# Residual shifts added by accumulating DMAs, and ScalarE's copies of the fifth product placed ahead of a norm, in a two-layer graph network on one Trainium2 core

## The chip, the core and the metric

The kernel runs on one core of one Trainium2 chip. The core has five engines, each with its own instruction queue: TensorE (PE in the profile; PEld is its weight load), VectorE (DVE), ScalarE (ACT), GpSimd (POOL) and SyncE (SP), which here issues DMA transfers alone. ScalarE and GpSimd issue a few transfers as well. All engines work on the on-chip memory SBUF; TensorE writes its sums into the banks of PSUM, from which VectorE and ScalarE read.

The metric is the device time of one execution in microseconds (us), the median of several runs. Lower is better.

## What is computed

64 graphs of 256 nodes with 256 features pass through two layers. Layer 0 is a graph attention layer with two attention steps, a norm, a feed-forward block with relu and a second norm. Layer 1 is a relational attention with 8 heads, a norm, a feed-forward block with gelu and a last norm. Cut to what matters:

```python
# layer 0
h = _gat(x, adj, W1, a1, Fout)
h = _gat(h, adj, W2, a2, W2.shape[1])
h = _layernorm(residual + h, g_ln1, b_ln1)
residual2 = h
ff = jnp.matmul(jax.nn.relu(jnp.matmul(h, w_ff1) + b_ff1), w_ff2) + b_ff2
return _layernorm(residual2 + ff, g_ln2, b_ln2)
# layer 1
...
attn_out = out.transpose(0, 2, 1, 3).reshape(Bb, Nn, Dm) @ Wo + bo
x = _ln(src + attn_out, g1, beta1)
ff = jax.nn.gelu(x @ W1 + b1, approximate=False) @ W2 + b2
return _ln(x + ff, g2, beta2)
```

All is float32. Each `_layernorm` or `_ln` ends with `* g + b`: a scale and a shift for each of the 256 features.

## The kernel before

**Tiles.** Two graphs make a unit; there are 32 units. A unit's residual rows are a tile `y` of 128 partitions x 4 x 256 (four blocks `t` of 128 nodes, 512 KB). There are four such tiles, which are reused.

**The norm in three parts.** `norm` (L795) takes statistics of each block on VectorE and has GpSimd make 1/sqrt(var + eps), called `rs`. `applied_norm` (L811) makes the negative mean `nm` on VectorE and then applies both to each block, on ScalarE (L821) or, where it is told so, on GpSimd (L818). `affine` (L824) scales with `times` (L830) and shifts with `plus` (L833), each one VectorE instruction over the whole tile. The features that go on into the next matmul don't need `affine`: its scale and shift are folded into the weights. So `affine` serves the residual path alone, and `rb1`, `rb2` and `rb3` also hold the bias of the matmul that is added next. `rb4` belongs to the output.

| vectors | used on | added to the tile next |
|---|---|---|
| `rg1`, `rb1` | rows after the first norm of layer 0 | feed-forward output of layer 0 (L961) |
| `rg2`, `rb2` | rows after the second norm of layer 0 | attention output (L789) |
| `rg3`, `rb3` | rows after the first norm of layer 1 | feed-forward output of layer 1 (L961) |
| `rg4`, `rb4` | rows after the last norm | nothing: stored by SyncE (L1120) |

**The feed-forward blocks.** Each block's first matmul is done as seven products of quarters (Strassen's scheme in the form of Winograd), each in two halves `a` and `b`: `hidden_seven` (L835). A step's name is the product and the half. Products 2, 5 and 3 use one PSUM bank of their half (`h1b`), and ScalarE copies it out after each (L873); products 1, 6, 7 and 4 use another (`h1a`), which VectorE adds into the same place of `h1` (L876). Product 3 accumulates on top of 5 in the same bank, so 3 of a half waits for the copy of 5 of that half; 6 needs the copy of 3. Step `r` and `s` are the activation. The second matmul is seven products too: `HiddenOut` (L923), with quarter sums on VectorE (L939) and adds into `y` (L961).

**Turns.** `turn(y_, x_, z)` (L1144) works on three units at once: on unit `y_` in layer 1, on `x_` in the feed-forward block of layer 0, and on `z` in the two GAT steps. There are 32 turns. While three units are there, the order on TensorE, SyncE, VectorE and ScalarE is the order of the code; GpSimd's order is the scheduler's. The places that the change touches, in a turn's order:

- After the first norm of `x_` and its transposes (`normed_features`, L663), `times` with `rg1` (L1197); the shift with `rb1` comes much later (L1227), among the relu products.
- After the first norm of `y_` and its transposes: `affine` with `rg4`, `rb4` of the unit that waits to be stored, the store (`stored`, L1118), then the load of the next rows (L1281).
- The gelu products of `y_` (L1296 to L1303), with the second norm of `x_` applied in between: block 0 after `5a`, then `affine` with `rg3`, `rb3`, block 1 after `5b`, blocks 2 and 3 (on GpSimd) after `3a` and `3b`.
- After output product 3 of `y_`: `affine` with `rg2`, `rb2` of `x_` (L1337).

`normed_features` transposes 32 x 32 blocks on VectorE (L668) and then moves 16 blocks into place: four by GpSimd copies (L685, L677), twelve by transfers from SyncE, or six each from SyncE and ScalarE. At the second norm of `x_` (L1305), the transposes need all four blocks of the norm.

A check of the input at the end chooses a general path otherwise; it isn't taken here.

Of the kernel before, what the change touches and what calls it, by code (L numbers as in the profile page):

```python
# [12 lines left out]
ALU = mybir.AluOpType  # L13
# [372 lines left out]
def narrow_path(  # L386
# [13 lines left out]
    nc = tc.nc  # L400
# [102 lines left out]
    def row(v, name, t=None):  # L503
        n = v.shape[0]
        if t is None:
            t = const.tile([P, n], F32, name=name)
        nc.sync.dma_start(t, bass.AP(tensor=v.tensor, offset=v.offset, ap=[[0, P], [1, n]]))
        return t
# [41 lines left out]
    rg1, rb1, rg2, rb2 = row(g_g1, "rg1"), row(g_b1, "rb1"), row(g_g2, "rg2"), row(g_b2, "rb2")  # L550
# [10 lines left out]
    rg3, rb3, rg4, rb4 = row(t_g1, "rg3"), row(t_be1, "rb3"), row(t_g2, "rg4"), row(t_be2, "rb4")  # L561
# [101 lines left out]
    def normed_features(u, l, xn, natural=False, queues=(nc.sync,)):  # L663


        yt = work.tile([P, Q, KB, T, 32], F32, tag="yt", name=f"yt{u}_{l}", bufs=1)
        for t in range(T):
            mark["transposed"] = nc.vector.transpose(  # L668
                yt[:, :, :, t].rearrange("p q k r -> p k q r"),
                xn[:, t].rearrange("p (k q c) -> p k q c", k=KB, c=32))  # L670
        if natural:
            hT = work.tile([P, KB, TN], F32, tag="hT", name=f"hT{u}_{l}")
            to = hT.rearrange("c k (t a r) -> c (k t) a r", a=Q, r=32)
            for q in range(Q):
                for a in range(Q):
                    move = nc.gpsimd.tensor_copy if q == a else nc.sync.dma_start
                    move(to[q * 32:(q + 1) * 32, :, a], yt[a * 32:(a + 1) * 32, q].rearrange("c k t r -> c (k t) r"))  # L677
            return [hT[:, k] for k in range(KB)]
        hT = work.tile([P, Q, KB, T, 32], F32, tag="hT", name=f"hT{u}_{l}")
        n = 0  # L680
        for q in range(Q):
            for a in range(Q):
                to, at = hT[q * 32:(q + 1) * 32, a], yt[a * 32:(a + 1) * 32, q]
                if q == a:
                    nc.gpsimd.tensor_copy(to, at)  # L685
                else:
                    mark["placed"] = queues[n % len(queues)].dma_start(to, at)
                    n += 1
        return [hT[:, :, k].rearrange("p a t r -> p t a r") for k in range(KB)]
# [105 lines left out]
    def norm(u, l, y, blocks=range(T)):  # L795
        n, t0 = f"{u}_{l}_{blocks[0]}", blocks[0]
        bt = slice(t0, t0 + len(blocks))
        st = work.tile([P, T, 6], F32, tag="st", name=f"st{n}", bufs=1)
        mv = work.tile([P, T, 2], F32, tag="mv", name=f"mv{n}")
        rs = work.tile([P, T], F32, tag="rs", name=f"rs{n}")  # L800
        nm = work.tile([P, T], F32, tag="nm", name=f"nm{n}")
        for t in blocks:
            nc.vector.bn_stats(st[:, t, :], y[:, t, :])  # L803
            nc.vector.bn_aggr(mv[:, t, :], st[:, t, :])  # L804
        nc.gpsimd.tensor_scalar(rs[:, bt], mv[:, bt, 1], EPS, 0.0, op0=ALU.add, op1=ALU.add)  # L805
        nc.gpsimd.tensor_tensor(rs[:, bt], rs[:, bt], mhalf[:, bt], ALU.pow)  # L806
        if l == 3:
            nc.gpsimd.tensor_add(high[:, bt], high[:, bt], mv[:, bt, 0])
        return blocks, mv, rs, nm

    def applied_norm(y, blocks, mv, rs, nm, part=None, gpsimd=False):  # L811
        bt = slice(blocks[0], blocks[0] + len(blocks))
        if part is None or part[0] == blocks[0]:
            nc.vector.scalar_tensor_tensor(nm[:, bt], mv[:, bt, 0], -1.0, rs[:, bt],  # L814
                                           op0=ALU.mult, op1=ALU.mult)
        for t in part or blocks:
            if gpsimd:
                nc.gpsimd.tensor_scalar(y[:, t, :], y[:, t, :], rs[:, t:t + 1], nm[:, t:t + 1],  # L818
                                        op0=ALU.mult, op1=ALU.add)
                continue  # L820
            mark["normed"] = nc.scalar.activation(y[:, t, :], y[:, t, :], AF.Identity,  # L821
                                                  bias=nm[:, t:t + 1], scale=rs[:, t:t + 1])

    def affine(y, g_, b_):  # L824

        times(y, g_)
        plus(y, b_)

    def times(y, g_):
        nc.vector.tensor_mul(y, y, g_[:, None, :].to_broadcast(list(y.shape)))  # L830

    def plus(y, b_):
        nc.vector.tensor_add(y, y, b_[:, None, :].to_broadcast(list(y.shape)))  # L833

    def hidden_seven(u, l, hT, w, bi, func, d, tt):  # L835

# [281 lines left out]
    def stored(u, y, bt):  # L1118
        b = slice(G * u + bt.start // NB, G * u + bt.stop // NB)
        nc.sync.dma_start(out[b].rearrange("b (c p) f -> p (b c) f", p=P), y[:, bt, :])  # L1120

    def finish(u, y, b):

        normed(u, 3, y, range(b * NB, (b + 1) * NB))
        bt = slice(b * NB, (b + 1) * NB)
        affine(y[:, bt, :], rg4, rb4)
        stored(u, y, bt)
# [16 lines left out]
    def turn(y_, x_, z):  # L1144
        Y, X, Z = (g.get(u) for u in (y_, x_, z))
        hT, y = Y["hT"], Y["y"]
# [7 lines left out]
        def scores(n):  # L1154
            e[n] = weighted(y_, *quads[n], q, k_, Y["aT"])
# [20 lines left out]
        def first(names, ends=0):  # L1176

            if X:
                steps(names)
            else:  # L1180
                for _ in range(ends):
                    piece()
# [4 lines left out]
        with order:  # L1187
# [6 lines left out]
            key(1)  # L1194
            if X:
                X["hT"] = normed_features(x_, 0, X["y"])
                times(X["y"], rg1)  # L1197
            scores(0)
            if z + 1 < NG:
                load_x(z + 1)  # L1200
# [22 lines left out]
            first("5b 7a 3b ra 6b")  # L1223
            totals(2)
            first("4a 7b rb")
            if X:
                plus(X["y"], rb1)  # L1227
            scores(3)
            first("sa sb", 2)
            masks(3)  # L1230
# [19 lines left out]
            n = norm(y_, 2, y)  # L1250
# [16 lines left out]
            if X:  # L1267
                out(6)
                hT = normed_features(y_, 2, y, queues=(nc.sync, nc.scalar))
                out(3)  # L1270
                out.sums(3)
            else:
                piece()
                hT = to_features(y, f"h3T{y_}")
                hT = [h.rearrange("p (t a r) -> p t a r", t=T, r=32) for h in hT]
                affine(y, rg3, rb3)
            if waiting:
                affine(waiting[0][1], rg4, rb4)
                stored(*waiting.pop(), slice(0, T))
            if z + 1 < NG:  # L1280
                load_rows(z + 1)  # L1281
# [9 lines left out]
            second = hidden_seven(y_, 1, hT, w1s, b1, AF.Gelu, Y, tt.rearrange("p a n -> p (a n)"))  # L1291
            if X:
                out.add(4)
                n = norm(x_, 1, X["y"])
            h1 = Y["h1"] = work.tile([P, FB, TN], F32, tag="h1", name=f"h1{y_}_1", bufs=1)
            second("2a 1a 2b 1b")  # L1296
            for t, name in enumerate(("5a", "5b", "3a", "3b")):
                second(name)
                if X:
                    applied_norm(X["y"], *n, [t], t > 1)  # L1300
                if X and t == 0:
                    affine(y, rg3, rb3)
            second("6a 6b ra rb 7a 7b")  # L1303
            if Z:
                X["hT"] = normed_features(x_, 1, X["y"], natural=True)  # L1305
# [28 lines left out]
            Z["m"].shares()  # L1334
            Z["m"].scaled(F)
            out(3)
            affine(X["y"], rg2, rb2)  # L1337
            out(7)
            checked(z, Z["aq"])
            if z + 1 < NG:  # L1340
# [6 lines left out]
    waiting = []  # L1347

    with tc.manual_schedule(engines={mybir.EngineType.PE, mybir.EngineType.SP}):
# [33 lines left out]
        for u in range(NG):  # L1383
            turn(u, u + 1, u + 2)
# [54 lines left out]
```

## Time and profile before

| | |
|---|---|
| median of 4 runs | 3094.73 us (3093.86 to 3095.8) |
| the profiled execution's own time | 3092.24 us |
| its span, first to last instruction | 3090.6 us |
| granted TensorE clock | 0.993 |
| transfers, all queues | 113.77 MB, mean 37 GB/s |
| GpSimd's transfers (`software_dynamic`) | 2, of 512 KB each, at the start |
| shifts on VectorE (L833) | 130, of them 126 over 128 x 1024 and 4 over 128 x 512 |
| scales on VectorE (L830) | 130 |
| ScalarE's copies of products (L873) | 384, 584 ns each |

How it is read: a row of a timeline gives the start in us from the span's start, the time taken, engine, line, operation, the tile written and the tiles read, the shape, and how many instructions the row merges. In brackets stands how long the engine was idle before the row and what ended that. Matmuls overlap; a row of matmuls that follows another without a pause starts a little before the other ends. Issues of DMAs are listed with the median time from issue to landing.

### The profile page before, as it was taken

To read this page: it belongs to the slowest core of one execution; us is meant where nothing else is said; L and a number is where in the kernel's file an instruction comes from. 1 tells how busy PE (TensorE), PEld (TensorE's weight loads), DVE (VectorE), ACT (ScalarE), POOL (GpSimd) and SP (SyncE) were. 2 spreads that over 40 slices of the span, in tenths; PEclk is the share of its full clock that TensorE was granted. 3 is DMA by queue.
4 is the path that set the end of the run, shared out by engine and by line. 5 is a ranking of instruction groups with operands and counts; after the bars stand their busy time and mean duration, and the time that the engine had idled before them with its cause. 6 is when DMAs were issued, how large, how long until landed. Compare 5 with 4: busy or idle time off the path is not lost. (4 is left out here: it accounts for less than half of the span.)

```text
span 3090.6 us, 56427 instructions
## 1 busy us (share of the span) xinstructions
PE 3039.9 (98%) x21424; PEld 2332.3 (75%) x21424; DVE 2583.2 (84%) x4888; ACT 1603.9 (52%) x3212; POOL 653.8 (21%) x892
## 2 busy tenths in 40 slices
PE   7999999999999999999999999999999999999997
PEld 6677877777777778777778777778777787777766
DVE  4788888888888888888888888888888888888875
ACT  4455555555545545545555555555555555455542
POOL 3122121122121222211221211221212221112210
PEclk8999999999999999999999999999999999999998
DMA  5011111121111211111211111211112211111100
GB/s 149 13 37 37 33 38 28 41 44 33 35 39 25 44 41 35 35 34 31 44 37 34 36 30 39 44 35 34 39 25 44 44 32 36 39 25 37 23 13 15
DMA packets 428564, 113.77 MB, mean 37 GB/s; under 512 B 364760, under 2 KB 427648, under 8 KB 428288
## 3 DMA queue, kind: packets, MB, share of 16 engines
q1 hardware_dynamic: 417952, 102.66, 15.8%
q10 hardware_dynamic: 9280, 6.39, 0.9%
q8 instruction: 172, 2.82, 0.4%
q0 software_dynamic: 1056, 1.05, 0.1%
q14 instruction: 104, 0.85, 0.1%
HBM read 57.04 MB, written 16.78 MB: 24 GB/s over the span
## 5 line engine op out<-in xcount | busy, mean ns | idle before, releaser
L873 ACT COPY h<-h1b 128x512 f32<-128x512 f32 x384 | 224.4, 584 | 397.0 <-PE h1b L864 397.0
L1019 DVE TENSOR_TENSOR ea<-e,aT 128x1024 f32<-128x1024 f32 x256 | 308.8, 1236 | 60.5 <-ACT e L1014 60.5
L821 ACT ACTIVATE y<-y,nm,rs 128x256 f32<-128x256 f32 x450 | 238.5, 591 | 230.6 <-DVE nm L814 226.3
L876 DVE TENSOR_TENSOR h<-h1a,h 128x512 f32<-128x512 f32 x384 | 262.5, 686 | 95.0 <-PE h1a L864 92.0
L1014 ACT ACTIVATE e<-sp 128x512 f32<-128x512 f32 x512 | 264.4, 603 | 56.0 <-PE sp L1008 45.3
L1047 POOL TENSOR_TENSOR low<-low,rq 128x16 f32<-128x16 f32 x64 | 13.9, 217 | 1088.3 <-DVE rq L1046 1088.3
L685 POOL COPY hT<-yt 32x256 f32<-32x256 f32 x248 | 210.5, 849 | 65.0 <-DVE yt L668 57.3
L992 PE MATMUL vp<-wv,hT 128*128 128x512 f32 x480 | 214.0, 599 | 0.0
L803 DVE BATCH_NORM_STATS2 st<-y 128x6 f32<-128x256 f32 x512 | 204.2, 401 | 0.3
L961 DVE TENSOR_TENSOR y<-yf,y 128x256 f32<-128x256 f32 x448 | 182.1, 407 | 20.6 <-PE yf L953 20.2
L805 POOL TENSOR_SCALAR rs<-mv 128x4 f32<-128x4 f32 (+1 forms) x130 | 30.4, 234 | 786.0 <-DVE mv L804 763.5
L992 PEld LDWEIGHTS vp<-wv,hT 128*128 128x128 f32 x480 | 88.7, 190 | 110.4 <-issue 103.2
L833 DVE TENSOR_TENSOR y<-y,rb 128x1024 f32<-128x1024 f32 (+1 forms) x130 | 167.1, 1286 | 3.2
L981 ACT ACTIVATE q<-qp,cols 128x512 f32<-128x512 f32 x64 | 44.0, 688 | 241.2 <-PE qp L979 241.2
L907 ACT ACTIVATE h<-h,cols 128x512 f32<-128x512 f32 x256 | 167.0, 714 | 1.6 <-DVE h L876 1.1
L830 DVE TENSOR_TENSOR y<-y,rg 128x1024 f32<-128x1024 f32 (+1 forms) x130 | 162.0, 1247 | 3.4 <-ACT y L821 2.3
L1024 DVE TENSOR_TENSOR es<-e 128x1024 f32<-128x1024 f32 x128 | 155.6, 1216 | 0.0
L1008 PE MATMUL sp<-q,k 32*128 32x256 f32 x2048 | 147.3, 400 | 4.6 <-ACT k L981 2.9
L1008 PEld LDWEIGHTS sp<-q,k 32*128 32x128 f32 x2048 | 92.7, 184 | 77.3 <-issue 45.6
L677 POOL COPY hT<-yt 32x256 f32<-32x256 f32 x120 | 113.5, 946 | 166.6 <-DVE yt L668 162.9
L806 POOL TENSOR_TENSOR rs<-rs,mhalf 128x4 f32<-128x4 f32 (+1 forms) x130 | 141.7, 1090 | 7.9
L668 DVE STREAM_TRANSPOSE yt<-y 128x256 f32<-128x256 f32 x368 | 131.7, 414 | 7.4 <-ACT y L821 6.8
(246 smaller groups left out, 7210.3 us busy)
## 6 DMA issues: line engine op xcount, KB each, us to landing
hT<-yt SPq DMA_DIRECT2D x918, 32.0 KB, 2.0
y<-in_x_dram SPq DMA_DIRECT2D x32, 512.0 KB, 4.5
xq<-in_x_dram SPq DMA_DIRECT2D x240, 64.0 KB, 2.2
aq<-in_adj_dram SPq DMA_DIRECT2D x240, 64.0 KB, 2.4
out_dram<-y SPq DMA_DIRECT2D x30, 512.0 KB, 2.9
hT<-yt ACTq DMA_DIRECT2D x186, 32.0 KB, 1.9
wf<-in_L_gnn_w_ff_dram SPq DMA_DIRECT2D x2, 1024.0 KB, 7.3
w<-in_L_gnn_W_dram SPq DMA_DIRECT2D x2, 1024.0 KB
```

The lines of the kernel that those rows point to most:

```text
L685: nc.gpsimd.tensor_copy(to, at)
L803: nc.vector.bn_stats(st[:, t, :], y[:, t, :])
L821: mark["normed"] = nc.scalar.activation(y[:, t, :], y[:, t, :], AF.Identity, bias=nm[:, t:t + 1], scale=rs[:, t:t + 1])
L833: nc.vector.tensor_add(y, y, b_[:, None, :].to_broadcast(list(y.shape)))
L873: mark["copied"] = nc.scalar.copy(out(h, o, b), pair(ps))
L876: mark["added"] = nc.vector.tensor_tensor(out(h, o, b), pair(one[h]), out(h, o, b), ALU.add)
L907: nc.scalar.activation(d["h1"][:, f, :], d["h1"][:, f, :], func, bias=bi[:, f:f + 1])
L961: nc.vector.tensor_tensor(yq, s.ps[n][:, :F].rearrange("p (i f) -> p i f", i=NB), yq, ALU.add)
L992: nc.tensor.matmul(ps, hT[k][:, t * P:(t + 1) * P], wvf[:, k, :], start=(k == 0), stop=(k == KB - 1))
L1008: nc.tensor.matmul(ps[a][:, j * N:(j + 1) * N], k_[hp, m, j0:j0 + P], q[hp, m, b * N:(b + 1) * N], start=True, stop=True)
L1014: mark[f"exp{b * KB + m}"] = nc.scalar.activation(e[:, a, :], ps[a], AF.Exp, scale=isd)
L1019: nc.vector.tensor_tensor(ea[:, a:a + 2, :], e[:, a:a + 2, :], ab[:, None, :].to_broadcast([P, 2, NB * N]), ALU.mult)
```

## The change

The shift can now be done by a DMA that adds its source, the row of 256 shifts repeated over four blocks, to the tile in SBUF. GpSimd issues it. It is used for the four shifts of a turn while `X` (the unit in layer 0's feed-forward block) is there; `rb2` in the turns that also have a unit `z`. The shifts outside of the turns, in the last turn and in `finish` stay on VectorE, and so does `rb2` in turn 30. The shift with `rb1` follows its scale at once instead of standing among the relu products. Among the gelu products, ScalarE's copies of `5a` and `5b` both stand ahead of the norm's first block, then `3a`, the second block, `3b`, and the last two blocks.

```diff
-    def affine(y, g_, b_):
+    def affine(y, g_, b_, dma=False):
         times(y, g_)
-        plus(y, b_)
+        plus(y, b_, dma)
...
-    def plus(y, b_):
-        nc.vector.tensor_add(y, y, b_[:, None, :].to_broadcast(list(y.shape)))
+    def plus(y, b_, dma=False):
+        b = b_[:, None, :].to_broadcast(list(y.shape))
+        if dma:
+            nc.gpsimd.dma_start(y, b, accum_op=ALU.add)
+        else:
+            nc.vector.tensor_add(y, y, b)
...
                 X["hT"] = normed_features(x_, 0, X["y"])
-                times(X["y"], rg1)
+                affine(X["y"], rg1, rb1, dma=True)
...
             first("4a 7b rb")
-            if X:
-                plus(X["y"], rb1)
             scores(3)
...
             if waiting:
-                affine(waiting[0][1], rg4, rb4)
+                affine(waiting[0][1], rg4, rb4, dma=X is not None)
                 stored(*waiting.pop(), slice(0, T))
...
-            for t, name in enumerate(("5a", "5b", "3a", "3b")):
-                second(name)
-                if X:
-                    applied_norm(X["y"], *n, [t], t > 1)
-                if X and t == 0:
-                    affine(y, rg3, rb3)
+            second("5a 5b")
+            if X:
+                applied_norm(X["y"], *n, [0])
+                affine(y, rg3, rb3, dma=True)
+            second("3a")
+            if X:
+                applied_norm(X["y"], *n, [1])
+            second("3b")
+            if X:
+                applied_norm(X["y"], *n, [2, 3], True)
             second("6a 6b ra rb 7a 7b")
...
             out(3)
-            affine(X["y"], rg2, rb2)
+            affine(X["y"], rg2, rb2, dma=True)
             out(7)
```

In the built program GpSimd's four issues of a turn stand: `rb1` behind the copies of L685 for `x_`'s first norm; `rb4` behind the copies of L685 for `y_`'s norm; `rb3` behind the norm's last two blocks (L818) and ahead of the copies of L677; `rb2` behind the reciprocals' sum of L755 and ahead of the next norm of `z` (L805). VectorE's order is otherwise the same, and TensorE's and SyncE's orders are the same.

## The prediction

> **What bounds the kernel now.** I read the page's busy times first, then the timelines of TensorE, ScalarE, VectorE, GpSimd and SyncE for two neighbouring turns (one from 1604.35 us, one from 1698.6 us) and for the turn before the last, then the DMA issues. The page:
>
> ```profile
> PE 3039.9 (98%) x21424; PEld 2332.3 (75%) x21424; DVE 2583.2 (84%) x4888; ACT 1603.9 (52%) x3212; POOL 653.8 (21%) x892
> ...
> L833 DVE TENSOR_TENSOR y<-y,rb 128x1024 f32<-128x1024 f32 (+1 forms) x130 | 167.1, 1286 | 3.2
> ```
>
> TensorE is busy 98% of 3090.6 us; L833, the operation that is replaced, is 167.1 us of VectorE. Busy time of pipelined matmuls hides short stalls, so I took the start of the first query matmul of each turn from the timeline. Of the 29 turns that start between 199 and 2822 us, 18 last 93.52 to 93.53 us; the other 11 lie above that by 4.1 us in sum. So TensorE runs at a floor, and a change off its path can win back little more than these 4.1 us. Eight of the 11 share one place, TensorE's third product of the gelu product. First the usual turn, then one of the eight:
>
> ```profile
> 1766.48 1.89 PE L864 MATMUL h1b<-tt,w1s 128*128 128x256 f32 x8
> 1768.20 2.08 PE L864 MATMUL h1b<-hT,w1s 128*128 128x256 f32 x8
> ```
>
> ```profile
> 1673.94 1.11 PE L864 MATMUL h1b<-hT,w1s 128*128 128x256 f32 x4
> 1675.28 1.13 PE L864 MATMUL h1b<-hT,w1s 128*128 128x256 f32 x4 [0.24 <-ACT h L873]
> ```
>
> Products 3a and 3b follow each other in the usual turn (eight matmuls in one row); here 3b starts at 1675.28 instead of 1673.94 + 0.94 = 1674.88. It accumulates into the bank that ScalarE's copy of 5b has yet to read, and that copy is behind the norm's first tile:
>
> ```profile
> 1674.16 0.60 ACT L821 ACTIVATE y<-y,nm,rs 128x256 f32<-128x256 f32 x1 [0.30 <-DVE nm L814]
> 1674.67 0.56 ACT L873 COPY h<-h1b 128x512 f32<-128x512 f32 x1
> ```
>
> **The reordered copies.** Product 5b ends at 1672.21 + 1.89 = 1674.10. Its copy, now ahead of the norm's tile, runs to about 1674.69 instead of 1675.23; 3b no longer waits. The eight turns exceed the floor by 0.53, 0.87, 0.52, 0.13, 0.76, 0.30, 0.30 and 0.28: 3.7 us. Turn 0 has the same wait, 0.3 us. In the usual turn 5b's copy ended at 1769.10 and 3b started at 1769.15; ending 0.12 earlier, it lets the weights be loaded a little sooner, some 0.02 us in 22 turns: 0.5 us. The norm's tiles move behind: 5b 1768.40, first tile 1768.86, 3a 1769.37, second tile 1769.83, 3b 1770.34 (steps of 0.46 to 0.51 as in the trace), where 3b's copy had 1770.32. So gelu does not move, and the transposes that read the norm's tiles start only at 1774.64.
>
> **VectorE's shifts.** 31 (rb1) + 30 (rb4) + 31 (rb3) + 30 (rb2) = 122 of the 130 go: 122 x 1.286 = 157 us of VectorE. On the path they are worth almost nothing, since after each one VectorE waits for somebody else:
>
> ```profile
> 1639.03 1.21 DVE L833 TENSOR_TENSOR y<-y,rb 128x1024 f32<-128x1024 f32 x1
> 1640.65 2.36 DVE L1019 TENSOR_TENSOR ea<-e,aT 128x1024 f32<-128x1024 f32 x2 [0.41 <-ACT e L1014]
> ...
> 1664.65 1.30 DVE L833 TENSOR_TENSOR y<-y,rb 128x1024 f32<-128x1024 f32 x1
> ...
> 1668.37 0.42 DVE L847 TENSOR_TENSOR tt<-hT 128x256 f32<-128x256 f32 x1 [2.08 <-DMA hT<-yt]
> ```
>
> ```profile
> 1768.92 1.47 DVE L833 TENSOR_TENSOR y<-y,rb 128x1024 f32<-128x1024 f32 x1
> 1771.26 0.69 DVE L876 TENSOR_TENSOR h<-h1a,h 128x512 f32<-128x512 f32 x1 [0.87 <-PE h1a L864]
> ...
> 1779.72 0.41 DVE L961 TENSOR_TENSOR y<-yf,y 128x256 f32<-128x256 f32 x1
> ...
> 1787.06 1.23 DVE L833 TENSOR_TENSOR y<-y,rb 128x1024 f32<-128x1024 f32 x1
> ...
> 1790.56 0.69 DVE L789 TENSOR_TENSOR y<-ygp,y 128x512 f32<-128x512 f32 x1 [0.20 <-PE ygp L786]
> ```
>
> Behind rb1 it waits for an exponential, behind rb4 for transfers, behind rb3 and rb2 for TensorE. The stretch where TensorE does wait for VectorE in every turn (0.26 us, the quarter sums before 1663.34) starts from an idle VectorE at 1652.17 and holds no L833. One place gains, the turn before the last:
>
> ```profile
> 2977.43 2.05 PE L953 MATMUL yf<-wf2t,h 128*128 128x128 f32 x16 [0.95 <-DVE y L961]
> ```
>
> There rb4's shift (2975.74 to 2976.96) stands ahead of the add that TensorE waits for; the product to be added ended at 2974.43 + 2.05 = 2976.48, so TensorE gains about 0.45 us.
>
> **The four transfers a turn.** Each carries 512 KB, issued by GpSimd in its queue behind the scale (L830). No run so far shows an accumulating transfer. The nearest rows:
>
> ```profile
> y<-in_x_dram SPq DMA_DIRECT2D x32, 512.0 KB, 4.5
> ...
> out_dram<-y SPq DMA_DIRECT2D x30, 512.0 KB, 2.9
> ...
> first<-in_adj_dram POOLq DMA_DIRECT2D x2, 512.0 KB, 7.8
> ```
>
> Issue took GpSimd 0.90 us (L462, two of them), and the 1 KB packets of that queue 61 ns each (the trace's packet records), 32 on each engine: 2.0 us. Lower bound from issue to landing: 2.9. Upper: the longer of GpSimd's two, 8.2, plus a second read (2.0) and a further pass (2.0): 12.2. The 7.8 comes from the crowded first 11 us, so I take the steady load, 4.5 + 0.9 for GpSimd's issue + 2.0 for the second read = 7.4.
>
> Who waits, and how long each may last:
> - rb3 is the tight one. GpSimd's queue puts it behind the norm's last two tiles:
>
> ```profile
> 1767.86 2.95 POOL L818 TENSOR_SCALAR y<-y,rs,nm 128x256 f32<-128x256 f32 x2 [0.31 <-DVE nm L814]
> 1776.19 3.87 POOL L677 COPY hT<-yt 32x256 f32<-32x256 f32 x4 [5.38 <-DVE yt L668]
> ```
>
>  It is issued at 1770.81; the add of 1779.72 must wait for it: 8.9 us. Behind this add VectorE holds the softmax, and TensorE has 0.4 us to spare there (GAT sums at 1786.90, second scaled tile at about 1786.48). So a landing after 9.3 us costs every us of excess 30 times. 7.4 costs nothing.
> - rb4: issued at 1666.2 behind GpSimd's copies; SyncE's store waits, then the row load that waits for the store, then the twelve moves of 1682.60: 1666.2 + 7.4 + 0.5 + 2.9 = 1677.0, 5.6 us in hand.
> - rb1 and rb2 are first read 39 and some 50 us later.
> - GpSimd's next work behind rb3 comes after 5.38 us of idleness, behind rb4 after 6.36, behind rb2 after about 6, behind rb1 after 15: an issue of 0.9 is covered.
>
> [...] No row of before shows an issue beside a busy VectorE.
>
> [...]
>
> **Sum.** 3.7 + 0.3 + 0.5 + 0.45 = 4.95 us off the profiled execution's 3092.24 (span 3090.6, 1.6 around it): 3087.3. That execution is 2.5 us quicker than the median 3094.73 of the four runs; taken off the median: 3089.8.
>
> **Rivals.**
> - More is won: the four runs' 2.5 us above the profiled one are more of the same wait of 3b, whose number varies with when the moves land. Then all runs fall to the floor, 3087.3. For: 18 turns agree to 0.01 us, so what varies must sit in such places. Against: nothing shows the other runs' turns.
> - Slower: rb3's landing. With GpSimd's own row, 7.8, and the second read, 2.0, it takes 9.8 us, 0.5 past the point: 30 x 0.5 = 15 less 5 gained, 3105. For: the only row of this queue. Against: it is from the start-up, when other queues moved over 1,800 packets beside it.
> - Nothing won: TensorE hides the shifts anyway, and rb4's 512 KB, which start while the last moves of hT land (1668.3), put back what the copies win; in the slow turns TensorE has 0.4 us there. About 3094.5.
>
> **How the numbers follow.** 6.2 us (0.2%) is about what a measurement of this kernel can tell from no change: faster is under 3088.5, slower over 3100.9. Forecast 0.55, between 3087.5 and 3092, of which 0.20 under 3088.5. More won 0.10. Nothing won 0.09. Slower 0.26. So faster 0.30, same 0.44, slower 0.26. The likeliest is 3089.8, its own range 3087.5 to 3092. The range of 3086 to 3106 holds all but half of the slower case and 0.05 below.
>
> **What would show it.** Right: no turn with 3b's wait; all turns at 93.5; transfers from L835 landing in 6 to 9 us; VectorE near 2425 us busy with more idleness in the same places. Wrong: VectorE waiting for the shift's transfer ahead of the first add of the second output product, GAT sums late, turns over 93.6; or GpSimd's issue over 5 us, so that its copies of hT come late; or turns below 93.5, which would mean that the floor was not TensorE's.

## The result, and the profile after

The changed kernel took 3102.94 us (median of 40 runs, 3093.4 to 3111.91) beside 3094.64 us for the kernel before (60 runs, 3091.41 to 3097.97): a ratio of 1.0027, 95% interval 1.0023 to 1.0032. It is 8.3 us slower, where 4.9 us were to be gained. Its runs also spread over 18.5 us, against 6.6 before. The profiled execution took 3094.34 us, 8.6 under its kernel's median: its lines show what happens, but less of it than usual. No execution near the median was profiled, so the size of the loss is read from the timed runs below.

From the page, in order: the span, the busy times, GpSimd's queue (packets, MB, share of 16 DMA engines), the new line's group (busy us, mean ns | idle before), and its transfers (KB each, us to landing):

```profile
span 3092.7 us, 56732 instructions
...
PE 3040.7 (98%) x21424; PEld 2334.7 (75%) x21424; DVE 2435.0 (79%) x4766; ACT 1602.6 (52%) x3212; POOL 761.8 (25%) x1014
...
q0 software_dynamic: 65472, 65.02, 13.3%
...
L835 POOL DMA_DIRECT2D y<-rb x122 | 162.2, 1329 | 50.9 <-ACT hp L766 49.1
...
y<-rb POOLq DMA_DIRECT2D x122, 512.0 KB, 5.3
```

The change does what it says. VectorE is relieved of 148 us (2583.2 before), GpSimd gets 122 issues of 1.33 us, and the transfers land in 5.3 us. TensorE is as busy as before (3040.7 us, 3039.9 before), so none of VectorE's 148 us comes back as time.

The copies do what they were moved for. Turn 16 had 3b's wait before; here are the same products of the changed kernel (TensorE's timeline), then ScalarE's in the same stretch:

```profile
1673.80 1.89 PE L868 MATMUL h1b<-tt,w1s 128*128 128x256 f32 x8
1675.53 1.75 PE L868 MATMUL h1b<-hT,w1s 128*128 128x256 f32 x7
```

```profile
1675.72 0.59 ACT L877 COPY h<-h1b 128x512 f32<-128x512 f32 x1 [0.28 <-PE h1b L868]
1676.21 0.60 ACT L821 ACTIVATE y<-y,nm,rs 128x256 f32<-128x256 f32 x1
```

The row of 3a and 3b runs on without a bracket, and 5b's copy stands ahead of the norm's tile. No turn has 3b's wait any more, and the shortest turn fell from 93.52 to 93.44 us.

The time is lost earlier in the same turn. First an undisturbed one of the changed kernel, turn 18, which starts at 1793.00; the rows are from the timelines of SyncE, GpSimd, VectorE and TensorE:

```profile
1850.49 3.92 SPq L687 DMA_DIRECT2D hT<-yt  x6
1853.92 1.34 POOL L835 DMA_DIRECT2D y<-rb  x1
1855.79 0.43 DVE L851 TENSOR_TENSOR tt<-hT 128x256 f32<-128x256 f32 x1 [1.28 <-DMA hT<-yt]
1857.41 1.03 PE L868 MATMUL h1b<-hT,w 128*128 128x256 f32 x4
```

And turn 16, which starts at 1604.51:

```profile
1661.99 4.94 SPq L687 DMA_DIRECT2D hT<-yt  x6
1665.42 1.34 POOL L835 DMA_DIRECT2D y<-rb  x1
1670.08 0.42 DVE L851 TENSOR_TENSOR tt<-hT 128x256 f32<-128x256 f32 x1 [4.06 <-DMA hT<-yt]
1670.27 1.10 PE L868 MATMUL h1b<-hT,w 128*128 128x256 f32 x4 [1.19 <-DMA hT<-yt]
```

In turn 18 the moves of `hT` land 62.8 us into the turn (VectorE's wait ends there), and TensorE comes to product 2a, which reads them, at 64.4. In turn 16 SyncE needs 4.94 us in place of 3.92 to issue its six moves, they land at 65.6, and TensorE waits. In the kernel before, VectorE's wait in this turn was 2.08 us, and TensorE did not wait here in any turn from 1 to 29. Two things happen just then. The packet records show that rb4's packets start 62.8 to 63.1 us into the turns (63.6 and 63.7 in 20 and 27). And a packet of 16 KB of the instruction queue (172 in the run, each about 1 us on one DMA engine) starts 60.9 us into turn 16. Such packets fall 60.7 to 61.5 us into turns 2, 6, 9, 13, 16, 20 and 27 and 57.7 to 58.2 us into turns 3, 10, 17 and 24. The new waits 64 to 67 us into a turn are in 2, 9, 10, 13, 16, 20, 24 and 27; turns 3, 6 and 17 have a packet and no wait there. The kernel before has its packets in the same eleven turns.

So the first theory (called "collision" below): a packet of the instruction queue delays the issue of some moves; where these would have landed ahead of rb4's packets, they now share the DMA engines with them and land too late for 2a. Its rivals in the expectations: the clock theory (the transfers lower TensorE's granted clock, each by a like share), that the new order of the copies costs something itself, and the late landing of rb3.

### The profile page after: what moved, and what is told of

Its sections match the earlier page's. It is cut to its first block, busy times and chain, and to the rows that moved or that the text cites. A ratio compares the mean times of both kernels' runs of the same rounds, so it can differ in the third digit from the quotient of the medians.

```text
span 3092.7 us, 56732 instructions
## 1 busy us (share of the span) xinstructions
PE 3040.7 (98%) x21424; PEld 2334.7 (75%) x21424; DVE 2435.0 (79%) x4766; ACT 1602.6 (52%) x3212; POOL 761.8 (25%) x1014
## 5 line engine op out<-in xcount | busy, mean ns | idle before, releaser
L685 POOL COPY hT<-yt 32x256 f32<-32x256 f32 x248 | 183.5, 740 | 68.7 <-DVE yt L668 60.9
L805 POOL TENSOR_SCALAR rs<-mv 128x4 f32<-128x4 f32 (+1 forms) x130 | 30.4, 234 | 681.8 <-DVE mv L804 677.3
L835 POOL DMA_DIRECT2D y<-rb x122 | 162.2, 1329 | 50.9 <-ACT hp L766 49.1
L830 DVE TENSOR_TENSOR y<-y,rg 128x1024 f32<-128x1024 f32 (+1 forms) x130 | 162.0, 1247 | 3.4 <-ACT y L821 2.3
L677 POOL COPY hT<-yt 32x256 f32<-32x256 f32 x120 | 115.5, 962 | 148.7 <-DVE yt L668 139.6
```

The lines of the kernel that those rows point to most:

```text
L835: nc.gpsimd.dma_start(y, b, accum_op=ALU.add)
```

## The experiments

Each kernel was timed beside the kernel before, whose median was 3095.3 us beside e1 to e4, 3094.3 beside e5 to e8 and 3094.6 beside the others; so differences between kernels of two groups are uncertain by 1 us beyond their intervals. Times are medians; the ratio is to the kernel before, with its 95% interval. "Above the floor" is the sum over turns 1 to 29 of what a turn takes above the shortest of its kernel, in the profiled execution. The wait of a product in a turn is counted from the starts of the matmuls: by how much it starts later behind the matmul before it than in an undisturbed turn. That is about 0.17 us more than the idle time in a row's bracket.

```
kernel                               us        ratio                    above the floor
before                               3094.6                              4.2
after                                3102.9    1.0027 (1.0023, 1.0032)   7.5
e1  new order, no transfer           3087.3    0.9976 (0.9966, 0.9986)   1.7
e2  old order, four transfers        3113.4    1.0060 (1.0047, 1.0073)  23.0
e3  new order, rb1 rb2 rb3           3089.7    0.9981 (0.9972, 0.9990)   3.7
e4  new order, rb4                   3099.1    1.0014 (1.0005, 1.0023)  14.8
e5  as after, rb4 later              3089.1    0.9981 (0.9972, 0.9990)   2.8
e6  as e4, plain copy, unread        3099.7    1.0017 (1.0008, 1.0026)  14.4
e7  new order, rb2 rb3               3088.3    0.9984 (0.9975, 0.9993)   1.5
e8  new order, rb1                   3091.2    0.9991 (0.9982, 1.0001)   5.0
e9  as after, 26 transposes ahead    3101.2    1.0023 (1.0014, 1.0031)  14.5
e10 as after, 40 transposes ahead    3110.1    1.0041 (1.0028, 1.0054)  26.3
e11 as e1, 26 transposes ahead       3087.9    0.9977 (0.9968, 0.9985)   2.3
e12 as before, 26 transposes ahead   3095.4    1.0000 (0.9992, 1.0009)   5.0
```

### Which part costs

e1 undoes the transfers and keeps the new order of the copies (against the changed kernel):

```diff
-                affine(X["y"], rg1, rb1, dma=True)
+                times(X["y"], rg1)
...
+            if X:
+                plus(X["y"], rb1)
...
-                affine(waiting[0][1], rg4, rb4, dma=X is not None)
+                affine(waiting[0][1], rg4, rb4)
...
-                affine(y, rg3, rb3, dma=True)
+                affine(y, rg3, rb3)
...
-            affine(X["y"], rg2, rb2, dma=True)
+            affine(X["y"], rg2, rb2)
```

> All shifts stay on VectorE at their old places; only the order of the gelu copies and the norm's tiles is the new one. Collision theory (the accumulating transfers run into the moves of hT): the wait of product 3b is gone and nothing is given back, 4 to 5 us under before, about 3090. Rival, the order costs (the norm's tiles or gelu come late): at or over before, 3095 to 3103. Clock theory (the added transfers lower the granted TensorE clock): like the collision theory here, 3090, with the clock of before.

e2 keeps the transfers and undoes the order:

```diff
-            second("5a 5b")
-            if X:
-                applied_norm(X["y"], *n, [0])
-                affine(y, rg3, rb3, dma=True)
-            second("3a")
...
+            for t, name in enumerate(("5a", "5b", "3a", "3b")):
+                second(name)
+                if X:
+                    applied_norm(X["y"], *n, [t], t > 1)
+                if X and t == 0:
+                    affine(y, rg3, rb3, dma=True)
```

> All four shifts of a turn by accumulating transfers, with the old order of the gelu copies. Collision theory: the waits of the changed kernel plus 3b's wait, which grows with late moves: 4 to 8 us over the changed kernel, 3107 to 3111. Rival, the order costs: under the changed kernel, 3095 to 3099. Clock theory: the changed kernel plus 4 us, 3107.

e3 takes the changed kernel and gives rb4's shift alone back to VectorE; e4 gives back the other three, as e1 does, and leaves rb4's to the DMA.

```diff
-                affine(waiting[0][1], rg4, rb4, dma=X is not None)
+                affine(waiting[0][1], rg4, rb4)
```

> The changed kernel with rb4's shift back on VectorE; rb1, rb2 and rb3 by accumulating transfers. Collision theory: the waits for the second group of moves (64.6 us into a turn) are gone, those 19 to 25 us into a turn stay: 3091 to 3095. Clock theory: three quarters of the loss stay, (3103 - 3090) x 0.75 + 3090 = 3100. A late landing of rb3: 3103 as in the changed kernel.

> The new order of the copies, and rb4's shift alone by an accumulating transfer; the other three on VectorE. Collision theory: most of the loss is here, 3097 to 3102, with waits 64.6 us into some turns and none 19 to 25 us into a turn. Clock theory: a quarter of the loss, 3093. A late landing of rb3: no loss, 3090.

The order by itself gains 8 us, so it is not what costs. The four transfers with the old order cost 18 us, more than expected: e2 waits both at 2a and, seven us later, at 3b. Of the transfers, rb4's costs 11.8 us (e4 less e1) and the other three 2.4 (e3 less e1; less than expected, and the two intervals overlap), so the cost is neither spread evenly, as the clock theory has it, nor rb3's. e4 shows it per turn. The times below are when VectorE's first difference of the gelu product starts, in us into the turn, which is when the last moves of its first operands have landed; TensorE's 2a comes at 64.4. Turn 12 has no packet of the instruction queue near the moves, the others have one:

```
turn                   2      9      13     16     27     12
e1 (no transfer)       64.32  63.99  63.77  64.45  64.25  63.08
e4 (rb4)               66.59  66.89  65.42  64.84  66.49  63.09
after (all four)       64.55  64.99  65.32  65.57  65.82  63.10
```

The packet alone makes the moves 0.7 to 1.4 us late (e1 against its turn 12), and TensorE's slack of 1.3 us (64.4 less 63.1) takes most of that. With rb4's transfer, which adds nothing in turn 12, they come up to 2.9 us later still. Neither alone makes 2a wait more than 0.3 us in these rows: e1 waits 0.24 us in turn 16, e4 not at all in turn 12.

### Where rb4's transfer lies, and what it does

e5 is the changed kernel with rb4's transfer, and the store and load behind it, put behind GpSimd's square root for the second norm:

```diff
...
-                affine(waiting[0][1], rg4, rb4, dma=X is not None)
-                stored(*waiting.pop(), slice(0, T))
-            if z + 1 < NG:
-                load_rows(z + 1)
+                times(waiting[0][1], rg4)
...
+            if waiting:
+                if X:
+                    with behind("pow"):
+                        plus(waiting[0][1], rb4, dma=True)
+                else:
+                    plus(waiting[0][1], rb4)
+                stored(*waiting.pop(), slice(0, T))
+            if z + 1 < NG:
+                load_rows(z + 1)
```

> All four shifts go by DMA as in the change, but rb4's transfer, the store behind it and the load of the next rows are put behind the square root of the second norm, so the transfer starts some 8 us later in the turn, when the 12 moves of hT have landed. Collision theory: the moves are late no more, the cost of rb4's transfer goes, and what is left is the kernel with three transfers, 3089.7 us (3088 to 3092), with no wait of 1 us or more 65 us into a turn. Rival (a fourth transfer of 512 KB per turn costs what it costs wherever it lies, by GpSimd's issue or by the load on the DMA engines): 3099 to 3103. Second rival (the later load of the next rows and the later store cost on their own): over 3103, with waits on SyncE's queue.

e6 is e4 with another transfer of 512 KB at rb4's place: a plain one into `v`, which is dead there. The shift with `rb4` is left out in the turns.

```diff
-                affine(waiting[0][1], rg4, rb4, dma=X is not None)
+                times(waiting[0][1], rg4)
+                if X:
+                    with behind("moved"):
+                        nc.gpsimd.dma_start(v[:, :, :F], rb4[:, None, :].to_broadcast([P, T, F]))
+                else:
+                    plus(waiting[0][1], rb4)
```

> As the kernel in which rb4 alone goes by DMA (3099.1 us), but the transfer at its place is a plain copy of the same 512 KB into v, which nobody reads any more in that turn, and rb4's shift is left out. If what delays the moves is that an accumulating packet holds its DMA engine for 102 ns, where a plain one of 1 KB took 46 to 61 ns, about half of the 11.8 us or less is left: 3087 to 3094. If it is the mere presence of 32 more packets on each engine ahead of the moves, whatever they do: 3096 to 3101.

e5 settles the place. It makes the same transfers as the changed kernel and takes 3089.1 us, 13.9 less. Its turn 16 starts at 1601.83 (timelines of SyncE, GpSimd, VectorE, TensorE):

```profile
1659.32 5.36 SPq L687 DMA_DIRECT2D hT<-yt  x6
1672.02 1.36 POOL L835 DMA_DIRECT2D y<-rb  x1
1666.50 0.43 DVE L851 TENSOR_TENSOR tt<-hT 128x256 f32<-128x256 f32 x1 [3.16 <-DMA hT<-yt]
1666.69 1.10 PE L868 MATMUL h1b<-hT,w 128*128 128x256 f32 x4 [0.28 <-PE yf L957]
```

SyncE's issue is even slower (5.36 us), so the packet of the instruction queue is there as before. But rb4's transfer is issued 9.3 us later in the turn, the moves land at 64.7, and TensorE is idle for 0.28 us in place of 1.19. The store and the load moved along with the transfer; at their old place, in e1, they cost nothing that shows.

e6 does not separate my two alternatives as they were meant, since its packets are not 32 of 1 KB. An accumulating packet of 1 KB takes 102 ns in the records; the plain copy went in eight packets of 4 KB on each engine, mostly 159 to 175 ns each, 1.3 us in all against 32 x 0.102 = 3.3 us. What it does show is that neither the accumulation nor the sum of the engines' time is what matters. Queue and transfer of e4, then of e6, from their pages:

```profile
q0 software_dynamic: 16896, 16.78, 3.3%
...
y<-rb POOLq DMA_DIRECT2D x30, 512.0 KB, 5.2
```

```profile
q0 software_dynamic: 5376, 16.78, 1.4%
...
v<-rb POOLq DMA_DIRECT2D x30, 512.0 KB, 3.7
```

Less than half of the engines' time, and the same cost: 3099.7 against 3099.1. The two spend it differently. In e6 GpSimd's issue is shorter (0.85 us against 1.36), so the packets start 62.35 us into the turn, not 62.85, and catch the moves in more turns: at 2a, turns 2, 3, 6, 9, 10, 13, 16, 20, 24 and 27 have waits of 0.8 to 1.6 us. In e4 three turns wait 2.1 to 2.3 us and four 0.6 to 1.1. The largest delay goes with the time that the transfer's packets take: against e1 the moves come 0.8 to 1.6 us later in turns 2, 9, 13, 16 and 27 of e6, where the packets start within 1.4 to 2.0 us, and 0.4 to 2.9 us in e4, where they start within 2.8 to 3.3 us.

e4's largest delay is 2.9 us, in turn 9; how the DMA engines share their time between the moves and the transfer stays open.

### The other three

e7 has rb2's and rb3's transfers alone, e8 rb1's alone, each with the new order. This is rb1's place in e8, against e1; the later `plus` goes:

```diff
-                times(X["y"], rg1)
+                affine(X["y"], rg1, rb1, dma=True)
...
-            if X:
-                plus(X["y"], rb1)
```

> New order of the copies, only rb2 and rb3 by DMA. No moves of hT are under way when these two run. Collision theory: no cost, 3087.3 us as with none (3086 to 3089). Rival (each transfer costs about 0.8 us over the run, three cost 2.4): 3088.9.

> New order of the copies, only rb1 by DMA; it runs beside the moves of the first product of the turn. Collision theory: rb1 is what the kernel with three transfers pays for, 3089.7 us (3088.5 to 3091), with waits 18 to 25 us into some turns. Rival (each transfer costs about 0.8 us): 3088.1.

e7 lies 1.0 us above e1 (2.1 when each is taken from the kernel before beside it), with overlapping intervals; its time does not decide against the rival's 3088.9. Its turns do: they show waits in the same places as e1's alone (1.5 us above the floor against 1.7). e8 is 4.0 above e1, more than expected: rb1's transfer starts beside the moves of the turn's first norm, and its profile has 2.2 us of waits 18 to 25 us into turns 3, 6, 13, 14, 20 and 27, which e1 has not. So rb1 seems to have the same fault as rb4, in a milder form. How much it costs is not settled: e3, which has rb1's transfer and two more, is quicker than e8 (3089.7 against 3091.2), with overlapping intervals.

### Is it the packet of the instruction queue?

That the late turns have such a packet may be a coincidence until it is moved. In the trace of the kernel before, 37 of them come in seven turns of 1328 recorded matmuls and weight loads each, so one for about 251; the expectation of e9 says 254. So extra instructions at TensorE's start shift them all. e9, e11 and e12 add 26 transposes of 8x8 ahead of TensorE's first wait, to the changed kernel, to e1 and to the kernel before; e10 adds 40 to the changed kernel. No turn is edited.

```diff
+        for _ in range(26 if name == "ga" else 0):
+            nc.tensor.transpose(ps[:8, :8], ident[:8, :8], ident[:8, :8])
         nc.tensor.transpose(ps[:, :at], rows[:at, :], ident[:at, :at])
```

> The changed kernel with 26 small transposes of 8x8 added at TensorE's start, before its first wait; nothing else. In the trace a 16 KB packet of the instruction queue comes every 254 matmuls and weight loads of TensorE, so 52 more instructions ahead move each packet that many instructions earlier in the program. Fetch theory (the moves of hT are late in those turns where such a packet falls among them, and rb4's transfer then catches them): by the times of the matmuls in the trace only turns 20 and 27 would still have a packet between 57.2 and 62 us, against 11 turns before; the waits of 0.2 us and more 64 to 67 us into the turn go in all other turns, and the time is 3089 to 3093 us. Rival (those turns are late for another reason, such as the rotation of the buffers): waits in turns 2, 9, 10, 13, 16, 20, 24, 27 as before, 3101 to 3105 us.

> As the kernel with 26 small transposes, but 40 of them (80 instructions). Fetch theory: the packets then fall 60.1 to 61.5 us into ten other turns, 1, 5, 8, 12, 15, 19, 22, 23, 26 and 29; the waits 64 to 67 us into a turn show in these and not in 2, 9, 10, 13, 16, 20, 24 and 27; 3100 to 3108 us. Rival: the same turns as in the changed kernel, 3101 to 3105.

> The kernel with the new order of the copies alone (all shifts on VectorE, 3087.3 us) with the 26 small transposes: what the 52 instructions cost by themselves and whether a late move costs anything there. Fetch theory: its two waits 64.6 us into turns 16 and 20 (0.5 us) go or move to other turns; 3086 to 3089 us.

> The kernel before with the 26 small transposes. Its waits 71 us into turns 2, 6, 9, 10, 16, 20, 24 and 27 (3.0 us) are what the new order of the copies removes. Fetch theory: these too come from moves that a packet of the instruction queue delays, so they show in turns 5, 12, 19, 23 and 26 instead, 1 to 2.5 us in all: 3092 to 3095 us. Rival (they belong to those turns): the same eight turns, 3094 to 3096.

The packets moved, and the waits went with them (turns 1 to 29):

```
        packets 57.5 to 61.6 us into turns       TensorE's waits for the moves, 64 to 68 us into turns
after   2 3 6 9 10 13 16 17 20 24 27             2 9 10 13 16 20 24 27
e9      2 5 9 12 16 19 23 26                     5 12 16 19
e10     1 5 8 12 15 19 22 23 26 29               1 5 8 12 15 19 22 23 26 29
        packets, the same stretch                TensorE's waits at 3b, 71 us into turns
before  2 3 6 9 10 13 16 17 20 24 27             2 6 9 10 16 20 24 27
e12     2 5 9 12 16 19 23 26                     5 9 12 16 19 23 26
```

Of these turns e10 hits the ten that were named, and no other. Turn 30 is not in the table: in e10 it has a packet 58.6 us in, and TensorE is idle for 3.21 us ahead of its 2a, longer than in any turn of the table. SyncE's issue of the six moves tells the same: in the changed kernel it takes 4.3 to 4.9 us in the eleven turns with a packet and 3.9 in the others (once 4.2), in e10 4.6 to 5.0 in its ten and 3.9 in the others. Why the issue itself takes longer is not shown. e10's rows of TensorE, first turn 16, which waits in the changed kernel and no longer here, then turn 12, which did not wait there:

```profile
1675.83 1.95 PE L959 MATMUL yf<-wf2t,h 128*128 128x128 f32 x16
1677.61 1.03 PE L870 MATMUL h1b<-hT,w 128*128 128x256 f32 x4
1678.48 1.03 PE L870 MATMUL h1a<-hT,w 128*128 128x256 f32 x4
```

```profile
1296.51 1.95 PE L959 MATMUL yf<-wf2t,h 128*128 128x128 f32 x16
1300.80 1.29 PE L870 MATMUL h1b<-hT,w 128*128 128x256 f32 x4 [2.35 <-DMA hT<-yt]
1301.89 1.91 PE L870 MATMUL h1a<-hT,w 128*128 128x256 f32 x4
1303.60 1.72 PE L870 MATMUL h1b<-hT,w 128*128 128x256 f32 x4
1305.15 1.03 PE L870 MATMUL h1a<-hT,w 128*128 128x256 f32 x4
```

For e9's time I was wrong. From the trace I had worked out that two turns would keep a packet near the moves; eight do, at 58.0 to 58.5 and 61.2 to 61.3 us, and it took 3101.2 us, not 3089 to 3093. The turns themselves answer: 5, 12 and 19 wait where the changed kernel did not, and 2, 9, 10, 13, 20, 24 and 27 no longer do. e11 shows that the transposes cost nothing measurable (3087.9 against 3087.3); its small waits at 2a left turns 16 and 20 for 5, 9 and 12, which have a packet. e12 moved 3b's waits, which the new order of the copies removes, to turns 5, 9, 12, 16, 19, 23 and 26, each of which has a packet, 3.3 us in all against 3.0; its time, 3095.4, is a little above what I expected. These waits too came from late moves.

## Why the prediction was wrong

- "TensorE runs at a floor": right. 157 us of VectorE's shifts were costed at almost nothing, and e7, which takes two of the four off VectorE and shows no new wait, is no faster than e1.
- "The reordered copies", 4.95 us with all that goes with them: right in kind, too small. e1 measured 3087.3 against 3095.3 for the kernel before beside it, 8.1 us. The mis-sized term is the earlier weight load, "some 0.02 us in 22 turns". In the usual turn of the kernel before, the first weight load of 3b waited 0.24 us for ScalarE's copy; in the changed kernel it does not wait. Every turn fell by 0.08 us, from 93.52 to 93.44: 29 x 0.08 = 2.3 us, not 0.5. The time above the floor fell from 4.2 to 1.7, 2.5 us, where 3.7 was taken off: turns 6, 16, 18 and 20 still have waits at other places. Together that is 4.8 of the 8.1 us; the other 3.3 were not traced. So it is not shown either that they are what the rival "more is won" had named, though its 3087.3 is e1's time. The 0.45 us of the turn before the last was there in the changed kernel (the add's wait fell from 1.12 to 0.69 us).
- Landing "4.5 + 0.9 + 2.0 = 7.4": 5.3 measured (5.1 to 7.3), nearer the plain load than the sum. GpSimd's issue, 0.90 by the start-up's row, was 1.33. That is not VectorE's doing: the issue takes 1.35 us for rb1 beside a VectorE that is busy all the time, and 1.32 for rb3, where VectorE is idle throughout in most turns; e6's plain copy takes 0.85. The longest of the 122 issues took 1.36 us. What made 1.33 of 0.90 is not shown.
- "rb3 is the tight one", the rival at 3105: refuted. It landed in time in every turn, and e7 with it costs nothing that shows. That 3105 is near the measured 3102.9 is chance.
- The step that failed is "rb4: ... 5.6 us in hand". I asked who waits for rb4's result, and that was right: nobody was late for it. I did not ask what its packets run into, except in the rival "nothing won", where rb4's 512 KB "start while the last moves of hT land" and "put back what the copies win", 4.95 us, with a chance of 0.09. That mechanism decided. It was mis-sized because I gave it 0.4 us in the slow turns of the profile and took these as they were, without asking why those turns were slow. The packets of the instruction queue stood in the trace of before, in the same eleven turns as in the changed kernel. So the term that the sum put at nothing is rb4's transfer beside the moves of `hT`: measured, it costs 11.8 us, and the other three together 2.4 more.
- With 8 us won by the order and 11.8 + 2.4 = 14.2 lost, the change would come to +6.1; measured are +8.3. The intervals, about 3 us to either side for each experiment, do not tell these two apart.

The fastest kernel is e1, the new order of the copies with all shifts on VectorE: 3087.3 us, 0.9976 (0.9966 to 0.9986) of the kernel before. Moving rb4's transfer behind the moves (e5) makes the transfers nearly free, but not useful.

## What to carry to other kernels

A transfer whose result nobody awaits soon can still have a price, 11.8 us for rb4's here: look up which transfers on the critical path are in flight when its packets start, and how much slack their reader has, 1.3 us here. Judge that slack in the slowest turns, and find out first why they are slow. When an engine is not the bound, work taken from it may buy nothing (e7, with two of VectorE's four shifts gone, took 3088.3 us against e1's 3087.3), so the place of what replaces it must be chosen as if it could only cost.

## What the hardware showed that I had not expected

- The instruction queue's packets disturbed data moves. In the turns where one of 16 KB fell among them, the moves of `hT` came late (by 0.7 to 1.4 us in the five turns of e1 in the table), and SyncE's issue of six moves took 4.94 and 5.36 us (turn 16 of the changed kernel and of e5) in place of 3.92. Which turns are hit changed with 26 small transposes at the very start of the program: in e9 turns 5, 12, 16 and 19 waited, in the changed kernel 2, 9, 10, 13, 16, 20, 24 and 27.
- A wait of 2.1 to 2.5 us of TensorE at 2a was followed by 3.4 us at half the granted clock in ten of the twelve cases in e2, e4, e9 and e10; waits up to 1.6 us were not. It shows in e10's turn 12 above: four matmuls take 1.91 us behind the wait, 1.03 later. What brings the clock down is not shown. Four such stretches, at a loss of 1.7 us each, make about 7 of the 10 us by which e10's ten waits, 16.2 us, become 26.3 above the floor.
- Of GpSimd's two scale-and-shift instructions of a turn (L818), the second went from 1.51 to 0.55 us when VectorE's shift with rb3 no longer ran beside it; the first, beside VectorE's scale (L830), stayed at 1.45. It is 0.55 in e7 too, where rb3 goes by DMA, and 1.51 in e4, where it does not.
